# A graph layer on one core: where VectorE reads its operands, how the edge selections are built, and how the mean is taken

## The chip, the cores and the metric

The kernel runs on one core of one Trainium2 chip. The metric is device time in microseconds: 3393.15 us is the median of three runs before the change (3389.51 to 3401.07). The profile is one further execution, taken by the hardware profiler; its span is 3650.9 us, longer than the timed runs, so its stages are read for their proportions and waits and not as the time itself.

Five engines work side by side, each through its own queue and in the order of that queue: TensorE (PE in the profile: matrix products, with PEld for the loads of weights), VectorE (DVE), ScalarE (ACT), GpSimd (POOL, which here issues the gathers) and SyncE (SP, which issues plain transfers). An engine that reaches an instruction whose input is not ready stands still, and everything behind it in its queue stands too.

## The reference

10,000 nodes with 512 features, 160,000 edges from `src` to `dst`, all in fp32. `xn = _layernorm(x)`, and the layer adds two branches to x and then a feed-forward part:

```python
x = x + gnn(xn) + mix(xn)
x = x + ffn(_layernorm(x))
```

The graph branch is `relu(segment_sum((xn @ W)[edge_src] * w, edge_dst) + bias)`. In the call the names are swapped, so that messages are gathered by the sorted index. The kernel sums the rows of xn first and multiplies by W afterwards, which gives the same.

The mixing branch is a linear attention with 8 heads of 64 features: `q = softmax(q, axis=-1) * scale` within each head of one node, `k = softmax(k, axis=-2)` over all nodes, `context = k^T v`, then `q @ context`, an output product, and a layer norm with a weight gamma.

The feed-forward part has 6 experts of 341 hidden features. Its router needs the mean over all nodes of the normalised x, `token_repr = x.mean(axis=1)`, and from it one weight for each expert; the output is the weighted sum of all experts.

## The kernel before

Nodes are cut into 20 chunks of 512 (the last has 272): a chunk is 128 partitions times `SUB` = 4 rows, called s below. The kernel has three long stages, and the order of TensorE's work in them is written out by hand (`manual_schedule` for PE). The other engines' queues are ordered by the framework's planner, which simulates the program and lets each instruction in when it expects its inputs.

**Keys and queries** (lines 745 to 794). Rows of xn are normalised and stored as `xn_d` in HBM. For each chunk, TensorE makes four products `pk` (keys) and four `pq` (queries), each of 128 rows by 512 features. ScalarE turns `pk` into `ek` and `pq` into `qt` by exponentials (L766, L773). VectorE then divides each head of the query by its sum in `softmax_rows`: sums of eight heads (L186), a reciprocal (L187), a product (L188). Afterwards TensorE turns the next chunk's rows, makes four products `pc` of keys with rows, which VectorE adds to `G` (L783), and turns `qt`. All of these products go through one pool of PSUM buffers, `ps`, with six buffers in rotation: an allocation waits for the one six before it to be read.

**Edges.** Beside the products runs the sum over edges, 1250 tiles of 128 edges each. `edges_in` issues one gather per tile from GpSimd (L483, `msg`) and lets VectorE build a selection `sel` for the tiles of one group, 8 tiles in the first part and 4 later: 31 columns per tile, in which an edge's weight stands at the place of its node. Two broadcast operations do that, a comparison (L489) and a multiplication by the weight (L492), and a small copy (L495) fills the remaining column. `edges_summed` multiplies messages and selections on TensorE (`pm`, L504), and ScalarE copies the sums to SBUF (L507), from where they go to HBM as `part_d`. The gathers go through 24 buffers. How many tiles are worked off beside each product is fixed by the constant `PACE`, in `work` (L598): 0.93 us of product for each tile.

**Nodes** (lines 888 to 962). For each chunk, `attention` makes four products `po` of the queries with the mixed context, normalises them (`row_stats`, then L907 and L909, which also add x), and leaves them in `ot`. `gathered` brings the edge sums of each node by an indirect transfer from GpSimd (L865, `at`), TensorE turns them to `aT`, and makes the four graph products `pg`. VectorE adds the bias to each (L933), putting the result into the tile of `at`, and then in one operation over all four rows takes the positive part and adds `ot` (L934). `row_stats` of `ot` follows. Then `normalize` writes the normalised rows over `at` (L178), and these are added to `xsum`, for the router's mean (L946). For the last chunk the normalised rows go to the tile of `wg`, and are added up by TensorE in `mean_row`.

**Experts.** About the last 1370 us are the feed-forward products (L1096), with the router's steps placed between the first of them.

The four places that the change touches are `softmax_rows` and its caller, the selection in `edges_in`, the node sums after `pg`, and `mean_row`.

Of the kernel before, what the change touches and what calls it, by code (L numbers as in the profile page):

```python
# [46 lines left out]
def gps_layer_kernel(  # L47
# [80 lines left out]
    gamma_b = const.tile([P, D], F32, name="gamma_b")  # L128
    nc.scalar.dma_start(gamma_b, gamma.to_broadcast([P, D]))
    row_of = const.tile([P, NCH, SUB], I32, name="row_of")  # L130
    stats2 = const.tile([P, NCH, SUB, 2], F32, name="stats2")


# [45 lines left out]
                o[:r, s, :], t[:r, s, :], mv[:r, s, 0:1], mv[:r, s, 1:2],  # L179
                op0=ALU.subtract, op1=ALU.mult)  # L180

    def softmax_rows(q, r, s):

        q3 = q[:r, s, :].rearrange("p (h e) -> p h e", e=HEAD)
        qs = small.tile([P, D // HEAD], F32, name="qs")
        nc.vector.tensor_reduce(qs[:r], q3, axis=AX.X, op=ALU.add)  # L186
        nc.vector.reciprocal(qs[:r], qs[:r])  # L187
        nc.vector.tensor_tensor(q3, q3, qs[:r, :, None].to_broadcast([r, D // HEAD, HEAD]), ALU.mult)  # L188

    def transposed(o, t, r, psum, tag, by_act=(1, 3)):  # L190

# [141 lines left out]
    with ExitStack() as ph:  # L333
# [139 lines left out]
        def edges_in(i):  # L473

            t0, batch = tiles_of(i)
            n = min(GROUP * batch, NET - t0)
            m = [None] * n
            for j in range(batch):
                for h in range(GROUP):
                    k = h * batch + j  # L480
                    if k < n:
                        m[k] = pools["m"].tile([P, D], F32, name="msg")
                        nc.gpsimd.indirect_dma_start(  # L483
                            out=m[k], out_offset=None, in_=xn_d,
                            in_offset=bass.IndirectOffsetOnAxis(ap=src_sb[:, t0 + k : t0 + k + 1], axis=0))
            sel = ew.tile([P, 2 * GROUP, WIN], F32, name="sel", bufs=6)
            if n < GROUP * batch:
                nc.vector.memset(sel[:, n:, :], 0.0)
            nc.vector.tensor_tensor(  # L489
                sel[:, :n, 1:], iota_w[:, None, :].to_broadcast([P, n, WIN - 1]),  # L490
                place[:, t0 : t0 + n, None].to_broadcast([P, n, WIN - 1]), ALU.is_equal)
            nc.vector.tensor_tensor(  # L492
                sel[:, :n, 1:], sel[:, :n, 1:],
                w_sb[:, t0 : t0 + n, None].to_broadcast([P, n, WIN - 1]), ALU.mult)
            nc.vector.tensor_copy(sel[:, :n, 0:1], on_w[:, t0 : t0 + n, None])  # L495
            return batch, m, sel

# [247 lines left out]
        for c, (_, r) in enumerate(chunks):  # L745
            if c == EARLY:
                normal_rows(NCH)
                place_edges()
                next_nodes()
                oddities()  # L750
                for soon in range(ROWS_SOON):
                    find_rows(soon, None)
                norm_ctx.close()
                done[1] = -6 * PACE
                pools["m"] = edge_ctx.enter_context(tc.tile_pool(name="edge_m", bufs=24,
                                                                 reuse_waits="tile"))
                nc.sync.dma_start(wv, w_qkv_t[:, 2 * D :].rearrange("(k p) d -> p k d", p=P))
                nc.sync.dma_start(wo, w_out_t.rearrange("(k p) d -> p k d", p=P))
            if c + 1 < NCH:
                xn_next = rows_of(c + 1)  # L760
            ek = b_io.tile([P, SUB, D], F32, name="ek")
            for s in range(SUB):
                pk = psum.tile([P, D], F32, name="pk", tag="ps")
                times(pk, xnT, s, r, wk)
                work(KB * PRODUCT)
                nc.scalar.activation(ek[:r, s, :], pk[:r], AF.Exp, scale=usable[:r])  # L766
                nc.vector.tensor_tensor(kacc[:r], kacc[:r], ek[:r, s, :], ALU.add)
            qt = b_io.tile([P, SUB, D], F32, name="qt")
            for s in range(SUB):
                pq = psum.tile([P, D], F32, name="pq", tag="ps")  # L770
                times(pq, xnT, s, r, wq)
                work(KB * PRODUCT)
                nc.scalar.activation(qt[:r, s, :], pq[:r], AF.Exp, scale=usable[:r])  # L773
                softmax_rows(qt, r, s)
            if c + 1 < NCH:
                xnT = turned_rows(c + 1, xn_next)
            for cb in range(KB):
                pc = psum.tile([P, D], F32, name="pc", tag="ps")
                for s in range(SUB):
                    nc.tensor.matmul(pc, ek[:r, s, cb * P : (cb + 1) * P], xn[:r, s, :],  # L780
                                     start=s == 0, stop=s == SUB - 1)
                if c:
                    added = nc.vector.tensor_tensor(G[:, cb, :], G[:, cb, :], pc, ALU.add)  # L783
                else:
                    nc.vector.tensor_copy(G[:, cb, :], pc)
                work(SUB * PRODUCT)
                if cb == KB // 2 - 1:
                    qT = b_io.tile([P, KB, SUB * P], F32, name="qT")
                    transposed(qT, qt, r, psum, "ps")
                    nc.scalar.dma_start(qT_d[c], qT[:, :, : SUB * r])  # L790
            if c >= ROWS_SOON:
                find_rows(c, added)
            if c + 1 < NCH:
                xn = xn_next
# [46 lines left out]
        wg = wq  # L841
        nc.sync.dma_start(wg, gnn_w.rearrange("(k p) d -> p k d", p=P))
        nc.vector.memset(xsum, 0.0)
        io = query_ctx.enter_context(tc.tile_pool(name="c_io", bufs=2, side="right", reuse_waits="tile"))

        def far_enough(c):
# [67 lines left out]
        for c, (_, r) in enumerate(chunks):  # L914
            ot, at = ot_next, held["at"]
            aT = io.tile([P, KB, SUB * P], F32, name="aT", bufs=1)

            def nodes_rows():
                transposed(aT, at, r, psum, "ps", by_act=range(KB))
                if c + 1 < NCH:  # L920
                    held["at"] = gathered(c + 1)

            if c + 1 < NCH:
                ot_next = attention(c + 1, nodes_rows)
            else:
                nodes_rows()

            et = at
            for s in range(SUB):
                po = psum.tile([P, D], F32, name="pg", tag="ps")  # L930
                times(po, aT, s, r, wg)
                put_out(KB * PRODUCT)
                nc.vector.tensor_tensor(et[:r, s, :], po[:r, :], bias_b[:r], ALU.add)  # L933
            nc.vector.scalar_tensor_tensor(ot[:r], et[:r], 0.0, ot[:r], op0=ALU.max, op1=ALU.add)  # L934
            nc.sync.dma_start(x1_d[c], ot[:r])
            mv = stats2[:, c]
            row_stats(ot, r, mv)

            nt = et if c < NCH - 1 else wg
            normalize(nt, ot, r, mv)  # L940

            nc.vector.scalar_tensor_tensor(mv[:r, :, 0], mv[:r, :, 0], -1.0, mv[:r, :, 1],
                                           op0=ALU.mult, op1=ALU.mult)
            if c < NCH - 1:
                for s in range(SUB):
                    nc.vector.tensor_tensor(xsum[:r], xsum[:r], et[:r, s, :], ALU.add)  # L946
            if c == NCH - 3:
                sums_of_weights()
            if c == NCH - 2:
                io_f["in"] = ctx.enter_context(tc.tile_pool(name="f_in", bufs=1, reuse_waits="tile"))  # L950

                io_f["squares"] = io_f["in"].tile([P, P // SQ, P], F32, name="squares")
                for b in range(P // SQ):
                    nc.vector.tensor_copy(
                        io_f["squares"][:, b].rearrange("k (g t) -> k g t", t=SQ),
                        ident[:, None, b * SQ : (b + 1) * SQ].to_broadcast([P, P // SQ, SQ]))
                xn = rows_in(0)
                st = small.tile([P, P // SQ, 1, SUB, 2], F32, name="st_sq", bufs=1)
                stats_of_squares(st, 0)
                for step in normalising(0, xn, st[:, :, 0]):  # L960
                    step()
                turn = turned_in(0, rows_turned(0, xn))
# [41 lines left out]
    def mean_row():  # L1004
        r = chunks[-1][1]
        nc.tensor.matmul(pmean, ones, xsum, start=True, stop=False)
        for s in range(SUB):
            nc.tensor.matmul(pmean, ones[:r], last[:r, s, :], start=False, stop=s == SUB - 1)
        mean_ctx.close()
        nc.vector.tensor_scalar(mean, pmean, 1.0 / N, None, op0=ALU.mult)  # L1010

    def mean_column():
        pr = psum_r.tile([P, D], F32, name="pr")
# [300 lines left out]
```

## Time and profile before

| what | value |
|---|---|
| timed runs, median | 3393.15 us |
| profiled span | 3650.9 us |
| TensorE busy | 3366.1 us |
| VectorE busy | 1701.6 us |
| ScalarE busy | 794.8 us |
| GpSimd busy | 1465.8 us |
| gathers of edges (L483) | 1250, mean 1004 ns |
| node sums (L934) | 20, mean 2295 ns |
| selection (L489 and L492, 8 tiles) | 112 each, mean 415 and 417 ns |
| product of the query softmax (L188) | 76 of 128 rows, mean 697 ns |

Busy time of an engine counts its instructions alone; what it needs between two of them is not in it. A group line of the profile names the line of code, the engine, the operation and the tiles it writes and reads, then the shape, the count, the busy time and the mean duration. In the timeline each line has a start, a length, engine and operation, and in brackets the idle time before it with the releaser that ended it; "issue" there is idle time for which no releaser was found. Stretches of the span are given as a row: the stretch, its length, the busy time of PE, PEld, DVE, ACT and POOL with the number of instructions, then the granted clock of TensorE, the busy share of the transfer engines, and GB/s.

### The profile page before, as it was taken

To read this page: it belongs to the slowest core of one execution; us is meant where nothing else is said; L and a number is where in the kernel's file an instruction comes from. 1 tells how busy PE (TensorE), PEld (TensorE's weight loads), DVE (VectorE), ACT (ScalarE), POOL (GpSimd) and SP (SyncE) were. 2 spreads that over 40 slices of the span, in tenths; PEclk is the share of its full clock that TensorE was granted. 3 is DMA by queue.
4 is the path that set the end of the run, shared out by engine and by line. 5 is a ranking of instruction groups with operands and counts; after the bars stand their busy time and mean duration, and the time that the engine had idled before them with its cause. 6 is when DMAs were issued, how large, how long until landed. Compare 5 with 4: busy or idle time off the path is not lost. (4 is left out here: it accounts for less than half of the span.)

```text
span 3650.9 us, 36451 instructions
## 1 busy us (share of the span) xinstructions
PE 3366.1 (92%) x12967; PEld 1946.6 (53%) x12967; DVE 1701.6 (47%) x3899; ACT 794.8 (22%) x1626; POOL 1465.8 (40%) x1472
## 2 busy tenths in 40 slices
PE   7999998989999858988988899999999999999998
PEld 3433333333333323333333334788888888888887
DVE  7723333333333324455545557554454454454542
ACT  4411111111111111112212121322222222222221
POOL 7666666656666655677776642000000000000000
PEclk9999999999999878999998899999999999999999
DMA  9676777767777676888888874122212212212210
GB/s 368 256 225 213 253 224 248 224 217 243 227 234 222 210 239 223 269 273 288 292 283 279 278 241 148 50 68 58 70 58 58 81 47 58 81 50 54 81 36 37
DMA packets 218326, 644.91 MB, mean 177 GB/s; under 512 B 35486, under 2 KB 75422, under 8 KB 193786
## 3 DMA queue, kind: packets, MB, share of 16 engines
q0 software_dynamic: 108208, 354.02, 31.6%
q1 hardware_dynamic: 67656, 168.51, 14.1%
q10 hardware_dynamic: 42266, 119.91, 8.6%
q8 instruction: 106, 1.74, 0.2%
q14 instruction: 90, 0.74, 0.1%
HBM read 485.32 MB, written 157.00 MB: 176 GB/s over the span
## 5 line engine op out<-in xcount | busy, mean ns | idle before, releaser
L483 POOL DMA_INDIRECT msg<-xn_d,src_sb x1250 | 1255.3, 1004 | 654.0 <-issue 291.1
L504 PE MATMUL pm<-msg,sel 128*32 128x512 f32 x2504 | 365.1, 620 | 49.0 <-issue 45.8
L203 PE MATMUL pg<-wq,aT 128*128 128x512 f32 (+1 forms) x640 | 313.9, 635 | 47.9 <-issue 40.0
L203 PE MATMUL po<-G,qT 128*128 128x512 f32 (+1 forms) x640 | 316.7, 638 | 29.2 <-issue 25.4
L780 PE MATMUL pc<-xn,ek 128*128 128x512 f32 (+1 forms) x640 | 307.5, 624 | 34.7 <-issue 19.2
L203 PE MATMUL pq<-wq,xnT 128*128 128x512 f32 (+1 forms) x640 | 288.4, 598 | 7.7 <-issue 6.5
L203 PE MATMUL pk<-wk,xnT 128*128 128x512 f32 (+1 forms) x640 | 285.7, 597 | 0.9 <-issue 0.8
L507 ACT COPY part<-pm 128x512 f32<-128x512 f32 x201 | 118.0, 587 | 741.4 <-remote 383.1
L203 PEld LDWEIGHTS pg<-wq,aT 128*128 128x128 f32 (+1 forms) x640 | 120.7, 197 | 242.3 <-issue 220.4
L203 PEld LDWEIGHTS po<-G,qT 128*128 128x128 f32 (+1 forms) x640 | 123.1, 199 | 211.7 <-issue 198.0
L504 PEld LDWEIGHTS pm<-msg,sel 128*32 128x32 f32 x2504 | 70.7, 110 | 306.0 <-issue 279.7
L780 PEld LDWEIGHTS pc<-xn,ek 128*128 128x128 f32 (+1 forms) x640 | 122.5, 199 | 192.0 <-issue 173.6
L489 DVE TENSOR_TENSOR sel<-iota_w,place 128x248 f32<-128x248 f32 (+2 forms) x201 | 71.4, 355 | 310.7 <-remote 202.5
L203 PEld LDWEIGHTS pq<-wq,xnT 128*128 128x128 f32 (+1 forms) x640 | 117.0, 187 | 179.3 <-issue 174.5
L1096 PE MATMUL px<-xnT,w_sb 128*128 128x256 f32 (+1 forms) x800 | 203.8, 377 | 9.2 <-DVE u L1131 8.9
L203 PEld LDWEIGHTS pk<-wk,xnT 128*128 128x128 f32 (+1 forms) x640 | 117.4, 187 | 166.0 <-issue 162.4
L1096 PE MATMUL px<-w_sb,hh 128*128 128x256 f32 (+1 forms) x800 | 185.7, 379 | 0.0
L1096 PE MATMUL py<-xs,w_sum 128*128 128x256 f32 (+1 forms) x800 | 185.6, 375 | 0.0
L1096 PE MATMUL py<-w_sum,hh 128*128 128x256 f32 (+1 forms) x800 | 179.2, 379 | 0.0
L160 DVE BATCH_NORM_STATS2 st<-ot 128x6 f32<-128x512 f32 (+1 forms) x160 | 106.7, 678 | 139.9 <-issue 79.1
L1096 PEld LDWEIGHTS px<-xnT,w_sb 128*128 128x128 f32 x800 | 150.3, 191 | 31.4 <-DVE u L1131 11.8
L1096 PEld LDWEIGHTS px<-w_sb,hh 128*128 128x128 f32 (+1 forms) x800 | 150.0, 188 | 22.7
(266 smaller groups left out, 4552.1 us busy)
## 6 DMA issues: line engine op xcount, KB each, us to landing
part_d<-part ACTq DMA_DIRECT2D x201, 256.0 KB
msg<-xn_d,src_sb POOLq DMA_INDIRECT x1250
xn<-in_x SPq DMA_DIRECT2D x19, 1024.0 KB
xn_d<-xn ACTq DMA_DIRECT2D x19, 1024.0 KB
qT_d<-qT ACTq DMA_DIRECT2D x19, 1024.0 KB
qT<-qT_d SPq DMA_DIRECT2D x19, 1024.0 KB
xt<-in_x SPq DMA_DIRECT2D x19, 1024.0 KB
x_d<-ot SPq DMA_DIRECT2D x19, 1024.0 KB
```

Of the source, the lines that this page charges most:

```text
L160: nc.vector.bn_stats(st[:r, s, :], t[:r, s, :])
L203: nc.tensor.matmul(po[:r, :], t[:, kb, s * r : (s + 1) * r], w[:, kb, :], start=kb == 0, stop=kb == KB - 1)
L483: nc.gpsimd.indirect_dma_start(out=m[k], out_offset=None, in_=xn_d, in_offset=bass.IndirectOffsetOnAxis(ap=src_sb[:, t0 + k : t0 + k + 1], ...
L489: nc.vector.tensor_tensor(sel[:, :n, 1:], iota_w[:, None, :].to_broadcast([P, n, WIN - 1]), place[:, t0 : t0 + n, None].to_broadcast([P, n ...
L504: nc.tensor.matmul(pm[h * WIN : (h + 1) * WIN, :], sel[:, k, :], m[k] if k < len(m) else m[0], start=j == 0, stop=j == batch - 1, skip_gro ...
L507: nc.scalar.copy(part, pm)
L780: nc.tensor.matmul(pc, ek[:r, s, cb * P : (cb + 1) * P], xn[:r, s, :], start=s == 0, stop=s == SUB - 1)
L1096: nc.tensor.matmul(o, lhs[j], rhs[j], start=start and j == 0, stop=stop and j == n - 1, skip_group_check=True)
```

## The change

It has four parts, all of which alter what VectorE is given.

*Query softmax.* ScalarE writes the exponentials back to the PSUM tile `pq`, and VectorE sums and multiplies from there; its product writes `qt` in SBUF as before. So the product has one operand in PSUM and one in SBUF, where it had two in SBUF.

*Selection.* One operation per tile, with the node's place and the edge's weight as two scalars per partition, does comparison and multiplication at once, on 31 columns. There are as many operations as tiles, where there were two per group.

*Node sums.* The bias is added in place in PSUM, and the positive part and the sum with `ot` are taken row group by row group, right after it, with one operand in PSUM.

*Mean.* The normalised rows are no longer made, save for the last chunk. Row x has the normalised value (x - m) / d; so the sum takes x times 1/d straight from `ot`, and the sum of -m/d, which is one number per row, is kept in `msum`, summed over partitions by one small matmul, and added to the mean at the end.

```diff
-    def softmax_rows(q, r, s):
+    def softmax_rows(q, r, s, e=None):
         q3 = q[:r, s, :].rearrange("p (h e) -> p h e", e=HEAD)
+        e3 = q3 if e is None else e[:r].rearrange("p (h e) -> p h e", e=HEAD)
         qs = small.tile([P, D // HEAD], F32, name="qs")
-        nc.vector.tensor_reduce(qs[:r], q3, axis=AX.X, op=ALU.add)
+        nc.vector.tensor_reduce(qs[:r], e3, axis=AX.X, op=ALU.add)
         nc.vector.reciprocal(qs[:r], qs[:r])
-        nc.vector.tensor_tensor(q3, q3, qs[:r, :, None].to_broadcast([r, D // HEAD, HEAD]), ALU.mult)
+        nc.vector.tensor_tensor(q3, e3, qs[:r, :, None].to_broadcast([r, D // HEAD, HEAD]), ALU.mult)
...
-            nc.vector.tensor_tensor(
-                sel[:, :n, 1:], iota_w[:, None, :].to_broadcast([P, n, WIN - 1]),
-                place[:, t0 : t0 + n, None].to_broadcast([P, n, WIN - 1]), ALU.is_equal)
-            nc.vector.tensor_tensor(
-                sel[:, :n, 1:], sel[:, :n, 1:],
-                w_sb[:, t0 : t0 + n, None].to_broadcast([P, n, WIN - 1]), ALU.mult)
+            for k in range(n):
+                nc.vector.tensor_scalar(sel[:, k, 1:], iota_w, place[:, t0 + k : t0 + k + 1],
+                                        w_sb[:, t0 + k : t0 + k + 1], op0=ALU.is_equal, op1=ALU.mult)
...
-                nc.scalar.activation(qt[:r, s, :], pq[:r], AF.Exp, scale=usable[:r])
-                softmax_rows(qt, r, s)
+                nc.scalar.activation(pq[:r], pq[:r], AF.Exp, scale=usable[:r])
+                softmax_rows(qt, r, s, pq)
...
-            et = at
             for s in range(SUB):
                 po = psum.tile([P, D], F32, name="pg", tag="ps")
                 times(po, aT, s, r, wg)
                 put_out(KB * PRODUCT)
-                nc.vector.tensor_tensor(et[:r, s, :], po[:r, :], bias_b[:r], ALU.add)
-            nc.vector.scalar_tensor_tensor(ot[:r], et[:r], 0.0, ot[:r], op0=ALU.max, op1=ALU.add)
+                nc.vector.tensor_tensor(po[:r, :], po[:r, :], bias_b[:r], ALU.add)
+                nc.vector.scalar_tensor_tensor(ot[:r, s, :], po[:r, :], 0.0, ot[:r, s, :], op0=ALU.max, op1=ALU.add)
...
-            nt = et if c < NCH - 1 else wg
-            normalize(nt, ot, r, mv)
+            if c == NCH - 1:
+                normalize(wg, ot, r, mv)
...
             if c < NCH - 1:
                 for s in range(SUB):
-                    nc.vector.tensor_tensor(xsum[:r], xsum[:r], et[:r, s, :], ALU.add)
+                    nc.vector.scalar_tensor_tensor(xsum[:r], ot[:r, s, :], mv[:r, s, 1:2], xsum[:r],
+                                                   op0=ALU.mult, op1=ALU.add)
+                moved = small.tile([P, 1], F32, name="moved")
+                nc.vector.tensor_reduce(moved[:r], mv[:r, :, 0], axis=AX.X, op=ALU.add)
+                nc.vector.tensor_tensor(msum[:r], msum[:r], moved[:r], ALU.add)
...
-        nc.vector.tensor_scalar(mean, pmean, 1.0 / N, None, op0=ALU.mult)
+        pr = psum_r.tile([P, D], F32, name="pr")
+        nc.tensor.matmul(pr[0:1, 0:1], msum, ones, start=True, stop=True)
+        shift = wp.tile([1, 1], F32, name="shift")
+        nc.vector.tensor_copy(shift, pr[0:1, 0:1])
+        nc.vector.tensor_scalar(mean, pmean, shift, 1.0 / N, op0=ALU.add, op1=ALU.mult)
```

More of the change, by code (lines that the diff above doesn't have):

```diff
@@ L130, in gps_layer_kernel @@
     row_of = const.tile([P, NCH, SUB], I32, name="row_of")
+    msum = const.tile([P, 1], F32, name="msum")
     stats2 = const.tile([P, NCH, SUB, 2], F32, name="stats2")
@@ L843, in gps_layer_kernel @@
         nc.vector.memset(xsum, 0.0)
+        nc.vector.memset(msum, 0.0)
         io = query_ctx.enter_context(tc.tile_pool(name="c_io", bufs=2, side="right", reuse_waits="tile"))
```

## The prediction

> **What bounds the kernel now.** I read the page's totals first, then busy time by stage, then GpSimd's gathers, then single stretches of the timeline.
>
> ```profile
> span 3650.9 us, 36451 instructions
> PE 3366.1 (92%) x12967; PEld 1946.6 (53%) x12967; DVE 1701.6 (47%) x3899; ACT 794.8 (22%) x1626; POOL 1465.8 (40%) x1472
> ```
>
> TensorE is busy 92% of the span and VectorE 47%, so work taken from VectorE is worth nothing as such. The whole-span shares hide that GpSimd works only until 2245 us. By stage (stretch, length, busy time of TensorE, weight loads, VectorE, ScalarE, GpSimd):
>
> ```profile
> 180.00:1270.00 1090.00, 1006.33 (x3608) 404.61 (x3606) 376.39 (x840) 180.14 (x294) 713.48 (x728) 0.97 0.73 228
> 1340.00:2160.00 820.00, 711.39 (x2298) 260.27 (x2297) 417.72 (x1105) 143.45 (x276) 556.12 (x537) 0.91 0.81 271
> 2160.00:2290.00 130.00, 119.74 (x371) 54.28 (x370) 94.43 (x198) 26.62 (x61) 24.93 (x70) 0.94 0.54 161
> 2290.00:3651.00 1361.00, 1342.11 (x6106) 1138.13 (x6105) 657.94 (x1332) 358.21 (x863) 0.00 (x0) 0.99 0.19 58
> ```
>
> Row one is the key and query stage, row two the node stage with edges, row three the last chunks and the passage to the experts, row four the experts. GpSimd's busy time leaves out what it needs between two gathers, which the timeline shows:
>
> ```profile
> 1562.15 0.94 POOL L483 DMA_INDIRECT msg<-xn_d,src_sb  x1 [0.30 <-issue]
> 1563.40 0.95 POOL L483 DMA_INDIRECT msg<-xn_d,src_sb  x1 [0.30 <-issue]
> 1564.41 2.29 DVE L934 SCALAR_TENSOR_TENSOR ot<-at,ot 128x2048 f32<-128x2048 f32 x1
> 1564.65 2.88 POOL L483 DMA_INDIRECT msg<-xn_d,src_sb  x1 [0.30 <-issue]
> ```
>
> A gather takes 0.95 us and the next starts 0.30 us later, although nothing is waited for: a period of 1.25 us. So GpSimd's floor is busy time plus 0.30 per gather: 713 + 728 x 0.30 = 931 us of 1090 in row one, 556 + 537 x 0.30 = 717 us of 820 in row two. TensorE's floor I take as busy time times granted clock: 1006 x 0.97 = 976 and 711 x 0.91 = 647. So TensorE binds the key stage with GpSimd 5% behind, and **GpSimd binds the node stage** by 70 us. The timed runs say that these floors are nearly met: they take 3393 us, 258 less than the profiled execution, and the floors take (1090 - 976) + (820 - 717) = 217 us off it. That the idle time above the floors is mostly absent from timed runs is my inference; no view shows it.
>
> The last two lines of that fence are the point of the case: a gather that starts while VectorE runs L934, with two operands in SBUF, takes 2.88 us instead of 0.95. Over all gathers:
>
> ```profile
> L483 POOL DMA_INDIRECT msg<-xn_d,src_sb x1250: 940/946/3132, 167.3 to 2157.7; - x179
> ```
>
> Half lie within 6 ns of the minimum, some take three times as long. I summed what each indirect transfer has over 0.946 us: 26 us in the key stage, 48 us in the node stage. Those that meet an L934 carry 22 us of the 48.
>
> [...] gathers that overlap L178 (fp32 tensor_scalar, 23 us of overlap) gain about 2 us in a least-squares fit of the excess on the overlaps.
> [...] The trace has 0.689 both for L933 (PSUM and SBUF) and L767 (SBUF alone): PSUM costs VectorE no more.
> [...]
> [...] The page shows granted clocks of 0.7 to 0.8 in slices of the node stage, and row two 0.91[...].
>
> **The change part by part.**
>
> *Node sums.* L934 (20 x 2.29 us, two SBUF inputs) becomes four operations of 512 per chunk that read one tensor from PSUM and one from SBUF. Those are not in the trace; bounds 0.69 (a PSUM tensor_tensor) and 0.75 (L907), I take 0.72, so 2.9 us for 2.29 a chunk. VectorE is about half busy in the stage: hidden. What counts is GpSimd: -22 us where it binds. The PSUM buffer is held 0.8 us longer; six allocations later comes its next user, which in the trace starts at least 5.8 us after L933 ends, so nothing waits.
>
> *Mean without normalised rows.* Out go 76 x 0.57 us (L178), worth some 2 us to GpSimd; the four xsum additions a chunk get a scalar (0.68 to about 0.75 us) and stay two-input: +1 us of contention. Two tiny additions a chunk, 0.3 us, hidden beside the matmuls. The buffer at comes free earlier; GpSimd waited 22.4 us in all for L946, mostly in the last chunks, where no gather of an edge follows; I count nothing. The mean gets one matmul, one copy and the wait between, about 0.5 us on the router's chain, which the first experts' matmuls mostly hide: +0 to 0.5.
>
> *Query softmax.* L188 with one input from PSUM stops contending: 5 us of the 26 by the fit, but in the stage that TensorE binds, so 0 to 3. Against it, pq stays in PSUM until the product is out: 0.69 + 0.20 + 0.69 us more (L186, L187, L188) plus hand-overs. Behind it is the buffer's next user, six allocations on: for the third and fourth pq of a chunk a matmul of pc. I took the end of each L188 from the trace against the start of that matmul: 13 of 80 come before the product's end by up to 4.4 us, the others mostly 2 to 8 us after it. Taking the worst of each chunk gives 13 us over the stage, 7 of them in the first three chunks; some vanish where VectorE is less late. I take +7, bounds 0 and 15.
>
> *Selection.* Per edge group two broadcast operations (0.415 + 0.417 for 8 tiles, 0.28 + 0.28 for 4) become 8 or 4 tensor_scalars on 31 elements with two pointer scalars. L178, of this form with 512 elements, repeats every 0.46 us; [...] 1.7 for 0.87 us and 0.84 for 0.6. Over 112 and 88 groups that is +93 and +21 us of VectorE, some 6% of the stages, with selections made several groups ahead: hidden. Contention: the old pair carries 13 us of the excess by the fit. [...] With L178's rate (2 us per 23 us of overlap) on about 165 us of overlap: 15 us. So 0, bounds -13 and +20.
>
> *Passage to the experts.* Here VectorE is the last:
>
> ```profile
> 2276.80 2.29 DVE L934 SCALAR_TENSOR_TENSOR ot<-at,ot 68x2048 f32<-68x2048 f32 x1
> 2285.22 0.42 DVE L1131 TENSOR_TENSOR u<-u,px 128x256 f32<-128x256 f32 x1
> 2285.70 1.65 PE L1096 MATMUL px<-xnT,w_sb 128*128 128x256 f32 x3 [4.47 <-DVE u L1131]
> ```
>
> TensorE waits 4.47 us for u, which stands in VectorE's queue behind the last chunk's sum, statistics and normalised rows. With sums and statistics taken per row group, three of four are done before the last product, so 2.29 + 3 x 0.85 - 0.72 = 4 us go: -4, all of it on the path.
>
> Sum: -22 - 1 (node stage) + 7 - 1 (key stage) + 0 - 4 = -21, hence 3372 us.
>
> **The rivals.**
> *Same:* GpSimd does not bind in timed runs, and its delays are made up in the gaps. For it: by the releasers GpSimd often waits for TensorE's pm to give back a buffer (172.6 us in all), and who waits for gathers is only 10 us of TensorE. Against it: the floors, and the 258 us. Then -4 and +4 remain: 3392 us.
> *Slower:* [...] +20 in place of 0, the PSUM holds cost their full 15, and stalls start half-clock windows: 3393 - 23 - 5 + 20 + 15 + some 15 = 3415 us. For it: "COPY sel" (L495) takes 126 to 587 ns[...]. Against it: the fit gives L495 next to nothing.
> *Faster still:* TensorE's waits on gathers shrink in step and with them the half-clock time. Row two at clock 0.91 loses 820 x 0.09 = 74 us; a third of it back is -25: 3347 us.
>
> **How the numbers follow.** Likeliest -21 (0.42), faster still 0.20, same 0.20, slower 0.18. The range takes in 3347 with ten us below for the selection's good bound, and above the same case and part of the slower one: 3336 to 3406. Faster by over 0.3% (under 3383): both faster cases less a tail, 0.60; same 0.20; slower 0.20.
>
> **What would show it.** Right: no gather over 2 us next to the node sums, the excess of the node stage near 25 us instead of 48, chunks of the node stage shorter. Wrong: gathers stretched to 1.1 or 1.2 us in bursts beside the selections; TensorE's pc waiting for VectorE's qt; the half-clock share growing; the wait of 4.47 us at the passage unchanged.

## The result, and the profile after

The changed kernel takes 3377.15 us (median of four runs, 3374.34 to 3381.44), the kernel before 3397.11 us beside it: ratio 0.9944, 95% interval 0.992 to 0.9969, or 20 us less. The forecast was 3372 us, 21 us less than the 3393.15 that it started from.

The result and the first four experiments come from chips on which the kernel before takes 3397 to 3399 us (medians), the other experiments, and by its pace the profile that the prediction reads, from chips on which it takes 3644 to 3662 us, so every ratio below is against the kernel before on the same chip. Differences in us are differences of medians.

The totals of the page after:

```profile
span 3379.6 us, 37367 instructions
PE 3270.7 (97%) x12969; PEld 1923.8 (57%) x12969; DVE 1842.5 (55%) x4771; ACT 797.3 (24%) x1626; POOL 1433.4 (42%) x1472
```

VectorE works 141 us more than in the profile of before (1701.6) and the kernel is faster: its busy time was not the limit.

For the stages a partner from a chip of the same pace is needed. This is the kernel before, run once more (e0 below); the rows are the first chunks, the key and query stage (first gather of an edge to first gather of node sums), the node stage with edges, the passage to the experts, the experts. Columns: stretch, length, busy time of TensorE, weight loads, VectorE, ScalarE, GpSimd, then the granted clock, the transfer engines' share, and GB/s.

```profile
20.00:190.00 170.00, 160.58 (x453) 75.20 (x454) 135.18 (x375) 72.79 (x115) 120.34 (x69) 0.97 0.80 301
172.00:1188.00 1016.00, 1000.53 (x3851) 418.62 (x3850) 401.04 (x900) 195.53 (x312) 766.98 (x776) 0.99 0.83 264
1188.00:1924.00 736.00, 700.23 (x2324) 256.93 (x2323) 426.06 (x1119) 147.40 (x284) 568.37 (x543) 0.98 0.90 306
1924.00:2023.00 99.00, 93.21 (x266) 39.02 (x265) 72.84 (x149) 18.34 (x44) 24.68 (x70) 0.97 0.61 174
2023.00:3400.00 1377.00, 1353.17 (x6145) 1147.44 (x6143) 668.32 (x1356) 360.40 (x867) 0.00 (x0) 0.99 0.19 59
```

The same stages of the kernel after:

```profile
20.00:190.00 170.00, 153.74 (x413) 71.82 (x414) 139.24 (x392) 71.63 (x113) 118.67 (x71) 0.94 0.78 294
170.00:1195.00 1025.00, 1011.15 (x3875) 423.58 (x3876) 502.25 (x1493) 194.87 (x314) 758.69 (x776) 0.99 0.83 262
1195.00:1904.00 709.00, 679.91 (x2336) 254.06 (x2335) 464.47 (x1378) 146.59 (x284) 537.39 (x547) 0.99 0.92 318
1904.00:2010.00 106.00, 94.09 (x254) 39.09 (x255) 73.54 (x154) 18.25 (x44) 21.85 (x67) 0.94 0.55 153
2010.00:3379.00 1369.00, 1348.89 (x6145) 1144.27 (x6143) 665.46 (x1351) 360.28 (x867) 0.00 (x0) 0.99 0.19 59
```

The node stage gives 27 us, the experts 8, and the stretches before and between take 9 and 7 back. GpSimd's floor (busy time plus 0.30 us per gather) is 568 + 543 x 0.30 = 731 us of 736 before and 537 + 547 x 0.30 = 701 of 709 after: GpSimd binds this stage in both, and its floor fell by 30.

The gathers of the kernel after, all 1250 (minimum, median, longest in ns):

```profile
L485 POOL DMA_INDIRECT msg<-xn_d,src_sb x1250: 943/949/2419, 169.9 to 1903.3; - x179
```

And one node sum with a gather beside it, in the timeline after (start, length, what):

```profile
1402.84 0.68 DVE L933 SCALAR_TENSOR_TENSOR ot<-pg,ot 128x512 f32<-128x512 f32 x1
1403.08 0.95 POOL L485 DMA_INDIRECT msg<-xn_d,src_sb  x1 [0.30 <-issue]
```

The gather starts 0.24 us into the sum and takes 0.95 us, where the same meeting cost 2.88 before. Over the node stage the gathers' excess over 0.946 us is 21.1 us (55.5 in e0), and only one takes over 1.8 us (21 in e0).

For the passage to the experts, the first products of the experts in e0, then in the kernel after (busy, mean ns | idle before them and its releaser):

```profile
L1096 PE MATMUL px<-xnT,w_sb 128*128 128x256 f32 x28 | 9.1, 458 | 4.5 <-DVE u L1131 4.5
```

```profile
L1103 PE MATMUL px<-xnT,w_sb 128*128 128x256 f32 x40 | 10.5, 384 | 1.8 <-DVE u L1138 1.8
```

The wait falls by 2.7 us, and the mean of a product from 458 to 384 ns: in e0 10.2 us at half clock begin at the wait (2031.9 to 2042.2), and the kernel after has none from 1998 to 2052.

The marks below say when TensorE reaches a point, in us; the brackets hold how much longer or shorter the step to it from the mark before became against e0. They are taken from the starts of TensorE's instructions; chunks are counted from 0.

```
                       e0      e1 (node sums)    after
first pm              195      196 ( +0.6)      207 (+11.7)
last pc              1124     1124 ( +0.0)     1136 ( +0.0)
first po             1174     1172 ( -2.5)     1180 ( -5.1)
pg of chunk 14       1834     1808 (-23.8)     1816 (-23.9)
last pg              2023     1994 ( -2.6)     2009 ( +3.8)
router's pe          2073     2038 ( -7.0)     2053 ( -6.9)
end                  3400     3364 ( -0.9)     3380 ( -0.5)
```

The long middle of the key stage is the same to 0.1 us. What is new is 11.7 us lost before the first pm, all of them in the first three chunks. A second, smaller loss stands before the last pg: 3.8 us where e1 gains 2.6. There TensorE waits 8.1 us for gathered messages in the kernel after, 2.8 in e1; why was not followed.

### The profile page after: what moved, and what is told of

Read it like the earlier page. It is cut to its first block, busy times and chain, and to the rows that moved or that the text cites. A ratio compares the mean times of both kernels' runs of the same rounds, so it can differ in the third digit from the quotient of the medians.

```text
span 3379.6 us, 37367 instructions
## 1 busy us (share of the span) xinstructions
PE 3270.7 (97%) x12969; PEld 1923.8 (57%) x12969; DVE 1842.5 (55%) x4771; ACT 797.3 (24%) x1626; POOL 1433.4 (42%) x1472
## 4 chain that ended last, share of the span: by engine, by line
PE 54%; DMA 9%; issue 1%; DVE 1%; POOL 1%; ACT 0%; POOLq 0%; DVEq 0%; ACTq 0%; SPq 0%
PE px L1103 15%; PE pz L1103 10%; PE py L1103 10%; PE po L205 7%; DMA msg<-xn_d,src_sb 6%; PE pg L205 6%; PE pm L503 3%; PE ph L1103 2%; PE pt L197 1%; DMA z_d<-xt 1%; POOL msg L485 1%; DMA xt<-x_d 1%; DMA at<-part_d,row_of 1%; DMA x_d<-ot 0%; PE pcarry L568 0%
## 5 line engine op out<-in xcount | busy, mean ns | idle before, releaser
L485 POOL DMA_INDIRECT msg<-xn_d,src_sb x1250 | 1226.5, 981 | 424.8 <-issue 236.6
L503 PE MATMUL pm<-msg,sel 128*32 128x512 f32 x2504 | 356.2, 603 | 28.7 <-DMA msg<-xn_d,src_sb 28.6
L492 DVE TENSOR_SCALAR sel<-iota_w,place,w_sb 128x31 f32<-128x31 f32 x1250 | 305.9, 317 | 103.9 <-PE pm L503 103.7
L205 PE MATMUL po<-G,qT 128*128 128x512 f32 (+1 forms) x640 | 292.7, 604 | 8.0 <-DMA qT<-qT_d 8.0
L205 PE MATMUL pg<-wq,aT 128*128 128x512 f32 (+1 forms) x640 | 293.5, 607 | 5.9 <-ACT aT L199 5.9
L779 PE MATMUL pc<-xn,ek 128*128 128x512 f32 (+1 forms) x640 | 288.7, 601 | 3.7 <-DVE qt L190 3.7
L205 PEld LDWEIGHTS po<-G,qT 128*128 128x128 f32 (+1 forms) x640 | 116.0, 189 | 171.0 <-issue 147.5
L1103 PEld LDWEIGHTS py<-w_sum,hh 128*128 128x128 f32 (+1 forms) x800 | 150.0, 188 | 22.7
```

The costliest lines, as they stand in the source:

```text
L205: nc.tensor.matmul(po[:r, :], t[:, kb, s * r : (s + 1) * r], w[:, kb, :], start=kb == 0, stop=kb == KB - 1)
L485: nc.gpsimd.indirect_dma_start(out=m[k], out_offset=None, in_=xn_d, in_offset=bass.IndirectOffsetOnAxis(ap=src_sb[:, t0 + k : t0 + k + 1], ...
L492: nc.vector.tensor_scalar(sel[:, k, 1:], iota_w, place[:, t0 + k : t0 + k + 1], w_sb[:, t0 + k : t0 + k + 1], op0=ALU.is_equal, op1=ALU.mult)
L503: nc.tensor.matmul(pm[h * WIN : (h + 1) * WIN, :], sel[:, k, :], m[k] if k < len(m) else m[0], start=j == 0, stop=j == batch - 1, skip_gro ...
L1103: nc.tensor.matmul(o, lhs[j], rhs[j], start=start and j == 0, stop=stop and j == n - 1, skip_group_check=True)
```

## The experiments

**e0, the kernel before once more,** unchanged, as the partner for traces.

> The kernel before, unchanged, profiled once more on the chip of the next runs. If its first profile, 258 us longer than its timed runs, held idle time that timed runs lack, this profile comes near 3395 us, the stretch of the node stage with edges shrinks from 820 us to about the 717 us that GpSimd needs, and the excess of its gathers over 0.946 us stays near 48 us there. If the idle time belongs to the kernel, it is 3600 us or more again.

Measured: 3402.46 us, span 3400.5. So profiling adds no 258 us of idle time. The profile in the prediction most likely comes from a slower chip: three further chips take 3644, 3647 and 3662 us for the same kernel in timed runs, with clocks near its 0.957 where e0 has 0.988. Which chip it was is not on record. In e0's trace the node stage takes 736 us, with an excess of 55.5 us (table above).

**e1, the node sums alone.**

```diff
-                nc.vector.tensor_tensor(et[:r, s, :], po[:r, :], bias_b[:r], ALU.add)
-            nc.vector.scalar_tensor_tensor(ot[:r], et[:r], 0.0, ot[:r], op0=ALU.max, op1=ALU.add)
+                nc.vector.tensor_tensor(po[:r, :], po[:r, :], bias_b[:r], ALU.add)
+                nc.vector.scalar_tensor_tensor(ot[:r, s, :], po[:r, :], 0.0, ot[:r, s, :], op0=ALU.max, op1=ALU.add)
```

> The kernel before with the node sums alone changed: bias added in place in PSUM, positive part and sum per row group with one operand in PSUM. The normalised rows, the selection and the softmax stay. [...] this part carries the gain, 18 to 24 us, ratio 0.993 to 0.995, no gather beside the sums over 1.2 us. Rival, less work for VectorE or a shorter passage: the normalised rows carry it, and this part gives at most the 4 us of the passage, ratio 0.998 to 1.0.

Measured: 3366.14 us, ratio 0.9911 (0.9893 to 0.9928), -33 us. Its node stage:

```profile
1186.00:1892.00 706.00, 685.03 (x2309) 254.61 (x2308) 438.51 (x1162) 145.43 (x281) 537.66 (x542) 0.99 0.92 318
```

706 us against 736, with a floor of 538 + 542 x 0.30 = 700: GpSimd binds, and freeing it pays one for one here (30 us of stage for 31 of floor). The 7 us at the passage come with this part too (marks above). In these runs this part alone gives more than the whole change.

**e2, the selection alone** (two broadcast operations per group become one tensor_scalar per tile, as in the diff).

> The kernel before with the selection alone changed, one operation with two scalars per tile. Theory: no difference, ratio 0.997 to 1.003, VectorE 120 to 170 us busier. Rival of the slower case: [...] ratio 1.004 to 1.01, with gathers stretched by 0.1 to 0.3 us beside them. Second rival: fewer two-input operations free GpSimd, ratio 0.994 to 0.997.

Measured: 3395.47 us, ratio 0.9986 (0.9979 to 0.9993), -4 us. The stages of e2, keys and nodes:

```profile
173.00:1191.00 1018.00, 1000.15 (x3845) 417.47 (x3843) 494.78 (x1484) 197.74 (x315) 761.83 (x776) 0.99 0.83 265
1191.00:1923.00 732.00, 695.38 (x2339) 257.09 (x2340) 466.16 (x1354) 145.72 (x282) 560.50 (x541) 0.98 0.90 307
```

VectorE has 94 and 40 us more than in e0, yet the gathers' excess falls, from 32.9 to 28.3 and from 55.5 to 49.5 us. The selection's own share shows in the gathers that start while one of its operations runs (and more than 0.12 us before its end): 79 of them have 8.1 us of excess in e0, 150 have 0.6 us in e2. The 1250 short operations with two pointer scalars hold GpSimd up less than the 402 broadcast ones that they replace.

**e3, the query softmax alone** (exponentials stay in `pq`, sums and product read them there).

> The kernel before with the query softmax alone changed, read from PSUM. Theory: TensorE binds this stage, so the longer hold of the PSUM buffers costs 0 to 7 us, ratio 1.0 to 1.003, with waits of TensorE's pc for VectorE's qt of up to 4 us in the first chunks. Rival: GpSimd binds here too, and the 5 us of contention it loses come back, ratio 0.997 to 0.999.

Measured: 3405.87 us, ratio 1.0016 (1.0008 to 1.0024), +6 us. TensorE's wait for `qt` is 2.1 us in the first 190 us, where e0 has none. One part of the change costs time by itself, but its trace shows only 1.3 us of the loss where it was looked for, before the first pm, and none in the rest of the key stage; the step to the last pg has 1.4 more and the experts 2.4, which the softmax does not touch.

**e4, the mean alone** (no normalised rows; scaled additions to `xsum`, and `msum`).

> The kernel before with the mean alone changed, no normalised rows save for the last chunk. Theory: 76 operations of 0.57 us less for VectorE, hidden; GpSimd gains 1 to 2 us, ratio 0.998 to 1.001. Rival, less work for VectorE is what counts: ratio 0.994 to 0.997.

Measured: 3641.89 us, ratio 0.9991 (0.9974 to 1.0007), on a chip that takes 3643.57 for the kernel before. The interval takes in 1, so no effect is shown.

**e5, the whole change with the old selection.**

> The changed kernel with the selection put back to two broadcast operations. Theory (the selection is neutral): as the changed kernel, ratio to the kernel before 0.993 to 0.996. Rival, the short operations cost: faster than the changed kernel, 0.988 to 0.992. Second rival, they carry part of the gain: 0.996 to 0.999.

Measured: 3640.13 us, ratio 0.999 (0.9976 to 1.0005), on the chip of e4. The interval takes in 1, so no gain is shown there. The whole change was not timed on that chip, so what the selection adds to it is not told by this. TensorE's waits for `qt` in the first 190 us are 6.7 us, as long as in the kernel after (6.6), though the selection is the old one. The first of them:

```profile
119.89 0.63 PE L197 MATMUL pt<-ident,xn 128*128 128x128 f32 x4 [3.36 <-DVE qt L190]
122.92 1.09 PE L197 MATMUL pt<-ident,xn 128*128 128x128 f32 x4 [2.40 <-DVE qt L190]
```

**e7 and e9, an extra operation in each chunk** of the changed kernel, over 2048 elements, whose result nothing uses: e7 reads two tensors in SBUF, e9 one.

```diff
+            nc.vector.scalar_tensor_tensor(at[:r], at[:r], 0.0, ot[:r], op0=ALU.max, op1=ALU.add)   # e7
+            nc.vector.tensor_reduce(extra[:r], at[:r].rearrange("p s d -> p (s d)"), axis=AX.X, op=ALU.add)   # e9
             nc.sync.dma_start(x1_d[c], ot[:r])
```

> The changed kernel with one extra operation on VectorE per chunk after the node sums: 2048 elements, both inputs in SBUF, result not used. It computes nothing that is kept. [...] gathers beside it stretch to 2 to 3 us, and 15 to 25 us of the gain are lost, ratio to the kernel before 0.998 to 1.002. Rival, VectorE's time counts: the same loss as with the one-input operation of the same length. Second rival, neither counts: 0.993 to 0.996 for both.

> The changed kernel with one extra operation on VectorE per chunk at the same place and of about the same length, a sum over 2048 elements of one tensor in SBUF, result not used. [...] gathers beside it keep their 0.95 us, ratio to the kernel before as the changed kernel, 0.993 to 0.997. Rival, VectorE's time counts: 0.998 to 1.002.

Measured, on the chip of e4: e7 3665.33 us, ratio 1.0072 (1.0044 to 1.0099); e9 3657.72 us, ratio 1.0034 (1.0019 to 1.005). The excess in the node stage is 38.6 us in e7 and 22.1 in e9. The timeline of e7, at one extra operation:

```profile
1775.79 2.28 DVE L934 SCALAR_TENSOR_TENSOR at<-at,ot 128x2048 f32<-128x2048 f32 x1
1775.81 3.08 POOL L485 DMA_INDIRECT msg<-xn_d,src_sb  x1 [0.30 <-issue]
```

And of e9, at one of its own:

```profile
1818.65 2.29 DVE L935 TENSOR_REDUCE extra<-at 128x1 f32<-128x2048 f32 x1 [13.93 <-DMA at<-part_d,row_of]
1818.80 0.95 POOL L485 DMA_INDIRECT msg<-xn_d,src_sb  x1 [0.30 <-issue]
```

Two inputs in SBUF stretch the gather, one does not: in the node stage 13 gathers that start during e7's operation have 19.1 us of excess, 27 during e9's have 0.05. Both times lie above what had been expected (0.998 to 1.002, and 0.993 to 0.997), e9's without any contention; what the changed kernel itself takes on this chip was not timed. Of the times only the order is told: the intervals overlap, and on this chip the node stage (825 us in e7, floor 714) is not at GpSimd's floor, so 16 us of contention need not show as 16 us.

**e6, rows one at a time, still in SBUF.** e1 changes two things: where the operand lies, and the length of the operation. e6 changes the length alone.

```diff
-            nc.vector.scalar_tensor_tensor(ot[:r], et[:r], 0.0, ot[:r], op0=ALU.max, op1=ALU.add)
+                nc.vector.scalar_tensor_tensor(ot[:r, s, :], et[:r, s, :], 0.0, ot[:r, s, :], op0=ALU.max, op1=ALU.add)
```

> The kernel before with its node sum cut into four operations of one row group each, as in the change, but still with both inputs in SBUF: the bias addition goes from PSUM to the buffer in SBUF, the relu and residual sum reads it there. The node sums of the change, measured by themselves, gave -33 us. Theory (it is the two SBUF inputs that hold GpSimd up): the node stage keeps its excess of about 50 us over 0.946 per gather, and only what comes from doing the rows one group at a time is won, some -7 us at the passage to the experts: ratio 0.997 to 0.9985. Rival (one operation of 2.29 us is the trouble, as it is long; four short ones let GpSimd in between): excess near 25 us, ratio near 0.991.

Measured: 3647.31 us against 3661.79, ratio 0.9946 (0.9925 to 0.9968), -14 us. The excess in the node stage is 29.3 us, where 50 had been expected of the theory and 25 of its rival; the ratio lies between the two. The step from the last pg to the router is 7.1 us shorter than in the first profile, so the gain at the passage comes from taking the rows one by one. A gather that meets one of the short operations, in its timeline, each line from the queue of its engine:

```profile
1560.14 0.69 DVE L934 SCALAR_TENSOR_TENSOR ot<-at,ot 128x512 f32<-128x512 f32 x1
...
1560.22 1.44 POOL L483 DMA_INDIRECT msg<-xn_d,src_sb  x1 [0.30 <-PE pm L504]
```

The gather that starts 0.08 us into the sum still waits, 0.49 us, so two inputs in SBUF do contend. But I paired all gathers of the node stage with the operations that they overlap, and what they show is finer than the theory: a gather already running when the operation starts was not slowed (50 such pairs in e6, excess at most 0.08 us); one that starts during it was held until about 0.12 us before its end. In the kernel before, a gather that starts 0.139 us into a sum of 2.291 has 2.029 us of excess: 2.291 - 0.139 - 0.123. (One that starts 0.04 us into a sum is not held; that sum takes 2.36 us.) A gather begins every 1.25 us, so an operation of 2.29 us always catches one, for 1.4 us on average (22.1 us over 16 sums in the first profile, which has e6's pace; 26.0 in e0), while one of 0.69 us catches about one in three and for 0.2 us (5.3 us over 64). Shortness won three quarters of the contention, PSUM the rest: in the kernel after, the 34 gathers that start during such a sum have 0.07 us of excess in all, and in e1, whose sums differ from e6's only in where one input lies, 33 have 0.17 us.

The same pairing over both stages, with gathers that start during an operation and more than 0.12 us before its end (how many, and their excess in us):

```
                    e0, before      after
node sums            16   26.0     29   0.05
query product        26    9.3     21   0.07
selection            79    8.1    149   0.8
```

Of the 46 us of excess left in the kernel after, 42 stand beside operations with two inputs in SBUF that the change leaves so: L449, L766, L907, L909 and the additions to `xsum`.

**e10 and e11, the whole change without the query softmax,** the same kernel on two chips.

> The whole change except the query softmax, which stays as before. Theory (the PSUM hold of the query softmax, together with VectorE being busier around it, costs the whole change about 12 us in the first three chunks): the time is that of the node sums alone or a little less, about 33 to 38 us under the kernel before, ratio 0.989 to 0.990, and the TensorE waits for qt in the first 215 us are gone. Rival (the selection or the mean, through the order of VectorE's queue, takes the node sums' gain back): as the whole change, about -20 us, ratio 0.994, with waits of TensorE in the first 215 us at other tiles.

> The kernel without the query softmax's part a second time, on the chip of this call. If this chip runs the kernel before in about 3397 us: -33 to -38 us, ratio 0.989 to 0.990, by the theory that the softmax's hold in PSUM costs the whole change some 12 us in the first three chunks; 0.994, as the whole change, by the rival that selection or mean gives the gain back. If it runs it in about 3645 us: as in the first run of this kernel, ratio about 0.996.

Measured: 3630.89 us, ratio 0.9962 (0.9944 to 0.9979), -16 us; and 3650.2 us, ratio 0.9964 (0.9949 to 0.9979), -12 us, as forecast for such a chip. Both chips were slower ones, so the forecast of 0.989 to 0.990 for a chip at 3397 us stays untried. Against e5 (0.999, on another chip), which has the softmax and lacks the selection, e10 is some 10 us better; that does not tell which of the two makes the difference.

**e12, selection and query softmax together.**

> The selection and the query softmax, without node sums and mean. Alone they measured -5 and +5 us. Theory (the two act on each other in the first three chunks, where VectorE has the selections of the first messages to make beside the statistics and the softmax): some 7 us more than their sum, +5 to +8 us, ratio 1.0015 to 1.0025, and the first pm comes about 12 us later than in the kernel before. Rival (they add up, and what costs the 12 us is the mean or the order made by the node sums): 0, ratio 0.9995 to 1.0005.

Measured: 3667.68 us, ratio 1.0065 (1.0044 to 1.0085), +21 us, on the chip of e10. More than expected of either theory. The first pm comes 26 us later than in the first profile, where 12 had been forecast. Who waits in the stretch from 40 to 190 us, in e12 (waited for: us in total, times, longest):

```profile
PE pt L196 <- DVE qt L189: 4.2, 3, 1.9
PE pc L778 <- DVE qt L189: 3.7, 2, 3.2
PE pt L196 <- DVE minus L365: 2.4, 1, 2.4
```

In e10, the same selection without the softmax:

```profile
PE pc L778 <- ACT qt L771: 1.8, 1, 1.8
PE pc L778 <- DVE G L781: 1.0, 1, 1.0
PE pt L196 <- DVE qt L189: 0.7, 1, 0.7
```

And the kernel after, TensorE's timeline where its first loss begins:

```profile
120.01 0.63 PE L197 MATMUL pt<-ident,xn 128*128 128x128 f32 x4 [1.86 <-DVE minus L366]
123.85 8.80 PE L779 MATMUL pc<-xn,ek 128*128 128x512 f32 x16 [3.21 <-DVE qt L190]
```

A matmul of `pc` waits 3.21 us until VectorE has read `pq` and its buffer comes free, and the 16 matmuls behind it take 8.80 us where 16 without a pause take 7.1 (e12, at 74 us): the granted clock was 0.58 from 124 to 128 us and 1.00 from 128 to 133. I summed by kernel the half-clock time from 40 to 190 us (part of it stands at the start in every kernel), TensorE's waits for VectorE's `qt` there, and how much later the fourth chunk's keys begin than in the kernel before, e0 for the faster chips and the first profile for the slower:

```
                             half clock   waits for qt   fourth chunk
e0, before                       5.4           0              0
e1, node sums                    3.8           0.7          +0.6
e2, selection                    3.1           0.7          -0.2
e3, softmax                      4.5           2.1          +1.3
after, all                      15.7           6.6         +11.7
first profile, before            2.9           0              0
e4, mean                         5.0           0.2          +1.8
e10, all but softmax             2.9           0.7          +4.3
e11, all but softmax             2.9           2.1          +4.1
e5, all but selection            9.9           6.7         +10.3
e12, selection and softmax      19.2           7.9         +17.8
e7, all, extra op later         16.3           7.1         +14.9
e9, all, extra op later         16.5           7.0         +15.7
```

Every kernel that loses 10 us or more has the softmax read from PSUM, and the softmax alone costs 1.3: it needs company. The selection is enough for that (e12), but it is not needed: e5 has the old selection, and node sums and mean, whose work begins only after 1100 us, are its only other changes. How they reach the first chunks is not shown. That the planner orders VectorE's queue otherwise for each kernel is my guess; in e0 and in the kernel after, VectorE is busy all of 100 to 127 us, so what is put ahead of a query there delays it.

## Why the prediction was right, point by point

*What binds.* GpSimd was held to bind the node stage, and TensorE the key stage. e0 shows both: floor 731 of 736, and a key stage whose middle is the same to 0.1 us in five kernels whatever GpSimd's excess. The argument for it was in part wrong: that timed runs lack the 258 us of idle time in the profile. Chips of the profile's pace take that long in timed runs too, and there the node stage (825 us, floor 724) is not at the floor. The conclusion held for the chip of the result, and would have been weaker for the other.

*Node sums, -22 and the passage, -4.* e1 gives -33, and its marks -24 over the node chunks up to chunk 14, -7 at the passage, and -5 in the two steps beside the node chunks. Mechanism and place are as forecast. The passage was sized too small: the wait fell by 2.7 us where 4 were counted, but the 10.2 us of half clock after it, about 5 us of work (half of it, an estimate), which the sum left out, went as well. The forecast put the hold-up down to the two inputs in SBUF, and took it that an operand in PSUM ends it; the first was read from L934 (2.88 against 0.95 us), the second was the author's assumption. e7 against e9 bears out the first, with 38.6 against 22.1 us of excess, and the kernel after the second, with 0.07 us for 34 gathers. e6 adds that a running gather loses nothing (at most 0.08 us in 50 pairs), and most of the 22 us comes from the operation's length. The order counts only one way in the traces: 14 sums of e0 that start beside a running gather last 2.29 us, like the others.

*Query softmax, +7 less 1.* e3 has +6 alone, right in size, but with 1.3 of it at the place forecast: the agreement is partly luck. In the whole change the first three chunks lose 12 us, against e1's 0.6. The forecast named that place (7 of 13 us in the first three chunks) and that sign (pc waiting for qt), and took each delay at its length; it missed that the loss depends on what else is changed, and that such waits, of up to 3.2 us, were followed by half-clock windows. The prediction counted on such windows in the node stage; that waits bring them on was the author's assumption there. In the kernel after, waits of 1.86 and 3.21 us close together are followed by a granted clock of 0.58 (124 to 128 us), and a single wait of 2.39 us by 0.50 (172 to 175 us); in the first profile the wait of 4.47 us at the passage is followed by 0.50 (2285.7 to 2290 us). In the first chunks 15.7 us at half clock in place of 5.4 is 5 us lost (half of the difference, an estimate), beside some 7 us more of waits for VectorE and ScalarE.

*Selection, 0.* The VectorE time was forecast at +93 and +21 us, from 1.7 us for eight operations and 0.84 for four, the author's estimates, which no view of before shows; e2 has +94 and +40. (The sum took the old pair at 0.87 and 0.60 us, where its parts make 0.83 and 0.56; that makes it +95 and +24.) The contention was taken as nil: counted at the excess fitted to L178, 2 us for 23 us of overlap, the new operations add 15 us, about the 13 that the old pair takes away. That they act like L178 was the author's assumption; 150 gathers that meet the new ones have 0.6 us, and in all the excess fell by 11 us, the time by 4. "Hidden" was right for the selection alone; beside the softmax e12 speaks against it.

*Mean, -1 to 0.* e4 agrees within its interval and proves no more.

So the total of -20 against -21 holds misses that cancel, and its closeness is luck: node sums and passage gave 33 where 26 were counted, and the first chunks cost about 12 where 7 were counted for the whole stage. The parts measured alone add up to -33 - 4 + 6 = -31 with the mean at nothing, 11 us more than the change gave; the interval of e1 alone is 6 us to either side. Against e1's trace, the kernel after loses 11 us more before the first pm and 6 before the last pg, and gains 3 at the first po. That the softmax has part in the first loss is shown by the table above. Which of the other parts it needs, and by which steps of VectorE's queue the delay builds up, is not, and the whole change was not timed on the slower chips.

Of the kernels tried, e1 is the best on the chip of the result's pace: 0.9911 against the change's 0.9944, though the ends of the intervals overlap (0.9928 and 0.992). The same on one chip would be needed to call it shown; the marks, 11 us apart at the first pm, speak for it.

## What to carry to other kernels

When another engine is held up by a VectorE operation with two inputs in SBUF, first cut the operation short: here that won three quarters of the contention that moving an operand to PSUM removed (in gather time, 22.1 us became 5.3; e6 and e1 ran on chips of different pace, so their times don't compare). A buffer in PSUM is not given back until its last reader is done (here `pc` waited 3.21 us for one), so look up who takes that buffer next and how full the reading engine is at just that time, not on average. And measure the parts of a change one by one: this gain of 20 us hid one part worth 33 and another that costs time beside the rest.

## What the hardware showed that was not expected

A gather already running was not slowed by a VectorE operation with two inputs in SBUF (at most 0.08 us in 50 pairs of e6); only those that start during it were held, until about 0.12 us before the operation's end (0.946 us became up to 3.08, in e7).

Operations of 31 elements with two pointer scalars last 317 ns each in the trace of the kernel after, and 1250 of them add 134 us to VectorE's busy time over the broadcast pairs (e2); yet they disturb gathers less, 0.6 us in place of 8.1.

Chips differ by 7 to 8% on the same kernel (3397 to 3399 against 3644 to 3662 us; mean granted clock 0.988 in e0, 0.957 in the first profile). Whether a change is worth the same on both was not measured: none was timed on both sorts. What makes these chips slower was not looked into.
